# Shorter edge lists and moved list transfers in a sparse graph attention kernel

## The chip, the cores and the metric

The kernel runs on one core of one Trainium2 chip. The metric is the device time of one execution in microseconds; less is better. Times of a kernel are given as the median of several runs with the lowest and highest beside it.

## What is computed

The reference is one layer of graph attention with a feed-forward part, on 4096 nodes of 512 features, 8 heads of 64. `adj` is a 4096 by 4096 matrix of int32 with ones where there is an edge; it is symmetric and its diagonal is one. Cut to what matters:

```python
hs = layer_norm(x);  ht = layer_norm(h_target)          # 4096 x 512 each
q, k, v = ht @ Wq + bq, hs @ Wk + bk, hs @ Wv + bv      # heads of 64
logits = where(adj != 0, q k^T / 8, -1e30)              # 4096 x 4096 per head
ht = ht + softmax(logits) v @ Wo + bo
ht = layer_norm(ht)
y  = ht + gelu(ht @ W1) @ W2                            # 512 -> 2048 -> 512
out = layernorm(x + y)
```

A row of `adj` has 17.05 ones on average, 5 at the least and 35 at the most (counted in the seeded inputs). So of the 4096 keys of a row only some 17 count, and the kernel never forms the dense logits: it makes a list of the neighbours of every row and gathers their keys and values.

## The kernel before

All tiles are 128 rows; there are 32 of them. The work has these parts.

**Projections.** Every tile of `x` is loaded through the sync queue, normalized, transposed on TensorE and multiplied by Wk and Wv (L930). ScalarE copies the result out of PSUM (L932), and a DMA of ScalarE's queue writes the 128 rows of keys and values, 512 KB, to a table `kvd` in DRAM (L936).

**Edge lists** (`edges`, L717 on). For each tile of 128 rows the adjacency comes in four quarter rows of 1024 int32, 512 KB each, by DMAs of the sync queue (`quarter`, L714). ScalarE turns a quarter into 1024 bytes of 0 or 1 and sums them to the row's degree (L729). VectorE reads the bytes as 512 pairs of 16 bits, multiplies each by its position in its segment, counted in columns (`lio`, L734), and takes the eight largest of every segment (MAX8, L736). A quarter row has `SQ` = 5 segments of at most 103 pairs (`WS`), so `SEG` = 20 segments a row give 160 candidates. At the end of a tile the low and high bytes of the candidates are taken apart (L743, L744), the offset of the segment is added where the byte is not zero (L748, L751), and from the 320 numbers the 24 largest are drawn by three MAX8 and two MATCH_REPLACE8 (L755, L757). They are the ids of the neighbours, plus one, and stand in the row's record. The rest of the 320 is written to DRAM (`rest_d`, L767, sync queue, in the middle of the next tile's edges) for the few rows with more than 24 neighbours, which read it back later (`rest_of`).

**Sorts.** The rows are sorted by degree in two halves (tiles 0 to 15 and 16 to 31), so that a tile of the sorted order needs only as many neighbour slots as its largest row (`CAPS_A`, `CAPS_B`; 11 to 39). `sort(part)` works out the rank of each row and scatters the records, 116 bytes each, of each of its 16 tiles to DRAM by an indirect DMA of GpSimd's queue (L854): 16 scatters in a sort.

**Attention.** For a sorted tile, `prefetch` loads the 128 records (L980, GpSimd's queue; six buffers, `rec`), asked for two tiles ahead. `front` gathers the rows of `h_target` and makes the queries. `issue` gathers the keys and values of one neighbour slot for 128 rows at a time (`gather`, L967: 603 of them for keys and values), three slots to a step, into a ring of 17, later 20, slots, four or five steps ahead. VectorE multiplies keys by queries (L1220) and sums them to logits (L1225), ScalarE takes the exponential (L1229) and scales one slot of the step (L1204), VectorE the other two (L1184), and TensorE adds the weighted values by transposes into PSUM (L1192), which frees the ring's slots. `finish` divides, multiplies by Wo, and normalizes.

**Feed-forward** (`feed`). Groups of two tiles go through W1 (L1325), Gelu on ScalarE (L1328) and W2 (L1334); `end` normalizes and scatters the rows to the output (L1302).

**Order.** Streams of the program are generators that `_weave` runs by costs: after each piece a stream tells a cost, and the stream with the smallest sum goes next. First the projections, the lists of the first 16 tiles with the first sort, and the lists of five more tiles (`fill`) are woven; then attention, feed-forward, and `other_lists` (the last 11 tiles' lists and the second sort). That gives the program order. A scheduler then orders each engine's queue when the kernel is compiled: by program order where instructions are ready in its own reckoning, so that a ready one may pass an earlier one that isn't. Each queue is executed in order: a waiting instruction holds what stands behind it. Gathers, scatters, the records' loads and a small power instruction (L687, for the normalizations) all stand in GpSimd's queue.

At its end the kernel checks flags (each row's count of ids against its degree, and the like). If one is set, a dense general path runs as well.

Of the kernel before, what the change touches and what calls it, by code (L numbers as in the profile page):

```python
# [1 line left out]

# [10 lines left out]
ALU = mybir.AluOpType  # L13
# [4 lines left out]
P = 128  # L18
# [360 lines left out]
RW = E0 + RE  # L379
# [5 lines left out]
def _order():  # L385


    n, m = len(CAPS_A), len(CAPS_B)
    a = [(k * P, c) for k, c in enumerate(CAPS_A)]
    b = [((n + k) * P, c) for k, c in enumerate(CAPS_B)]  # L390
    groups = [[a.pop()]]
    while len(a) > 1:
        groups.append([a.pop(), a.pop()])
    groups.append(a + [b.pop()])
    while len(b) > 1:
        groups.append([b.pop(0), b.pop()])
    return groups + [b]
# [46 lines left out]
def adj_resnorm_kernel(  # L444
# [33 lines left out]
    nc = tc.nc  # L478
# [9 lines left out]
    NQ = 4  # L488
    QW = N // NQ
    WQ = QW // 2  # L490
    SQ = 5
    WS = -(-WQ // SQ)
    SEGS = [(s * WS, min(s * WS + WS, WQ)) for s in range(SQ)]
    SEG = NQ * SQ
    groups = _order()
# [17 lines left out]
    recs_d = [dram.tile([n * P, RW], I32, name=f"rec{i}") for i, (_, n) in enumerate(PARTS)]  # L513
# [19 lines left out]
    with tc.tile_pool(name="keep", bufs=1) as keep:  # L533
# [17 lines left out]
        with ExitStack() as late:  # L551
# [50 lines left out]
            cnt = lp.tile([P, NT], F32, name="cnt")  # L602
            segoff = lp.tile([P, 2, NQ, SQ], F32, name="segoff")
            lio = lp.tile([P, WQ], U16, name="lio")
# [3 lines left out]

            def list_constants():
                io = turn_of("wide", wide)  # L610
                nc.gpsimd.iota(io[:, :SQ * WS], pattern=[[0, SQ], [2, WS]], base=1,
                               channel_multiplier=0)

                nc.vector.tensor_copy(lio, io[:, :WQ])
                io = turn_of("wide", wide)
                nc.gpsimd.iota(io[:, :2 * SEG], pattern=[[1, 2], [QW, NQ], [2 * WS, SQ]], base=0,
                               channel_multiplier=0)
                nc.gpsimd.iota(io[:, 2 * SEG:2 * SEG + NB], pattern=[[1, NB]], base=0,
                               channel_multiplier=0)

                nc.vector.tensor_copy(segoff.rearrange("p b q s -> p (b q s)"), io[:, :2 * SEG])
                nc.vector.tensor_copy(bins, io[:, 2 * SEG:2 * SEG + NB])

                nc.gpsimd.memset(lower, -1.0)
                nc.gpsimd.affine_select(out=lower, in_=lower, compare_op=ALU.is_ge, fill=0.0,
                                        base=0, pattern=[[-1, P]], channel_multiplier=1)
                for R, (i0, n) in zip(Rs, PARTS):
                    nc.gpsimd.memset(R, 0)
                    for c, base in ((TGT, i0 * P), (ROW, 0)):
                        nc.gpsimd.iota(R[:, :, c], pattern=[[P, n]], base=base,  # L630
                                       channel_multiplier=1)
                nc.vector.memset(one_c, 1.0)
# [76 lines left out]
            def quarter(i, h):  # L709
                if i < RINGED:  # L710
                    a = ring[:, (i * NQ + h) % DEEP, :].bitcast(I32)
                else:
                    a = turn_of("wide", wide)
                nc.sync.dma_start(a, adj[i * P:(i + 1) * P, h * QW:(h + 1) * QW])  # L714
                return a

            def edges(i):  # L717

                part = 1 if i >= NA else 0
                rec = Rs[part][:, i - PARTS[part][0], :]  # L720
                cand = lp.tile([P, SEG, 8], U16, name="cand", bufs=2)
                for h in range(NQ):
                    n = i * NQ + h
                    while len(adjs) < min(n + 2, NT * NQ):
                        adjs.append(quarter(*divmod(len(adjs), NQ)))
                    a, adjs[n] = adjs[n], None

                    sg = turn_of("signs", signs)
                    nc.scalar.activation(sg, a, AF.Sign, accum_out=dpart[:, i, h:h + 1])  # L729
                    ahead = min(n + DEEP - 1, n + 3 + n // 2)  # L730
                    while len(adjs) < min(max(n + 3, min(ahead, RINGED * NQ)), NT * NQ):
                        adjs.append(quarter(*divmod(len(adjs), NQ)))
# [12 lines left out]
                gid = lp.tile([P, 2 * SEG, 8], F32, name="gid")  # L745
                dec = dec.rearrange("p b s e -> p (b s) e")
                off = segoff.rearrange("p b q s -> p (b q s)")
                nc.vector.scalar_tensor_tensor(gid, dec, 0.0,  # L748
                                               off.unsqueeze(2).to_broadcast([P, 2 * SEG, 8]),
                                               op0=ALU.is_gt, op1=ALU.mult)  # L750
                nc.vector.tensor_add(gid, gid, dec)  # L751
                flat = gid.rearrange("p s e -> p (s e)")
                for r in range(RE // 8):
                    top = rec[:, E0 + r * 8:E0 + (r + 1) * 8]
                    nc.vector.max(top, flat)  # L755
                    if r + 1 < RE // 8:
                        nc.vector.match_replace(flat, top, flat, 0.0)  # L757
                held.append((rest_d[i * P:(i + 1) * P, :], flat))
                has = lp.tile([P, MAXE], F32, name="ehas")
                nc.vector.tensor_scalar(has[:, :RE], rec[:, E0:E0 + RE], 0.0, 0.0, op0=ALU.is_gt,  # L760
                                        op1=ALU.add, accum_out=cnt[:, i:i + 1])
                yield 4.0

            def keep_rest():

                while held:
                    nc.sync.dma_start(*held.pop())  # L767
# [40 lines left out]
            def sort(part):  # L808
# [3 lines left out]
                pool, R = lp, Rs[part]  # L812
# [3 lines left out]
                ranki, b16 = tools[:, 960:960 + n].bitcast(I32), tools[:, 976:984].bitcast(BF16)  # L816
                nc.vector.scalar_tensor_tensor(dif, deg[:, me], float(RE), cnt[:, me], op0=ALU.min,
                                               op1=ALU.not_equal)
                nc.vector.tensor_reduce(bad[:, 1 + part:2 + part], dif, AX.X, ALU.max)
                nc.vector.tensor_scalar(dif, deg[:, me], 0.0, float(NB - 1), op0=ALU.max,  # L820
                                        op1=ALU.min)
# [14 lines left out]
                for c in range(2):  # L836
# [5 lines left out]
                                                 op0=ALU.mult, op1=ALU.add)  # L842
# [8 lines left out]
                nc.vector.tensor_copy(ranki, rank)  # L851
                yield 10.0
                for i in range(n):
                    ins = nc.gpsimd.indirect_dma_start(  # L854
                        out=recs_d[part][:, :],
                        out_offset=bass.IndirectOffsetOnAxis(ap=ranki[:, i:i + 1], axis=0),
                        in_=R[:, i, :], in_offset=None)

                    tc.declare_no_dep(ins.ins, group=f"scatter{part}", reason="other rows")
                    tc.add_to_no_dep_group(f"scatter{part}", ins.ins)  # L860
                    yield 3.0 if part else 1.3
# [99 lines left out]
                        yield cost  # L961


            recs, tqs, h2Ts, done, ready, latest, newest = {}, {}, {}, set(), [], [], []

            def gather(dst, table, idx):
                nc.gpsimd.indirect_dma_start(  # L967
                    out=dst, out_offset=None, in_=table[:, :],
                    in_offset=bass.IndirectOffsetOnAxis(ap=idx, axis=0))

            def prefetch(i):
                if i >= NT or i in recs:
                    return
                r0 = TILES[i][0]
                part = 1 if r0 >= PARTS[1][0] * P else 0
                assert part in done
                r0 -= PARTS[part][0] * P
                rec = sp.tile([P, E0 + MAXE], I32, name="rec", bufs=6)

                nc.gpsimd.dma_start(rec[:, :RW], recs_d[part][r0:r0 + P, :])  # L980
                recs[i] = rec

            def front(i, idle=0):
# [503 lines left out]
```

## Time and profile before

| what | value |
|---|---|
| median of 3 runs | 1815.98 us (1813.75 to 1820.42) |
| profiled execution, its time | 1817.49 us |
| its span in the profile | 1815.5 us |
| TensorE matmul busy | 1677.8 us, 92% |
| VectorE busy | 1436.5 us, 79% |
| ScalarE busy | 1224.1 us, 67% |
| GpSimd busy | 982.2 us, 54% |
| mean granted TensorE clock | 0.967 |
| DMA | 463.26 MB, 255 GB/s on the mean |

The profile is that of one execution. A share of busy time is a mean over stages with different limits, so the stages are looked at one by one: the projections with the first lists up to some 296 us, the start of attention up to 380 us, attention beside the last 11 tiles' lists up to some 600 us, the second sort's scatters between 627 and 665 us, attention with feed-forward up to 1650 us, and the tail. In the lists below, "[a <-b]" after an instruction is the time that its engine sat idle before it, and what ended the wait. L numbers are lines of the kernel.

### The profile page before, as it was taken

How to read it: one execution, taken by the hardware profiler on the slowest of the kernel's cores; microseconds unless marked ns; L12 is line 12 of the kernel's file. 1: busy time of each engine (PE TensorE's matmuls, PEld its weight loads, DVE VectorE, ACT ScalarE, POOL GpSimd, SP SyncE). 2: the span in 40 equal slices, each digit the busy share in tenths (PEclk: the TensorE clock that was granted, in tenths of full speed). 3: DMA queues.
4: the chain of work that ended last, by engine and by line, in shares of the span. 5: the costliest groups of instructions: out<-in, count | busy, mean ns of one | idle time of the engine just before them, and what ended most of it. 6: DMA issues, size and time to landing. Idle time of an engine off the chain costs nothing. (4 is left out here: it accounts for less than half of the span.)

```text
span 1815.5 us, 22973 instructions
## 1 busy us (share of the span) xinstructions
PE 1677.8 (92%) x7030; PEld 1097.9 (60%) x7030; DVE 1436.5 (79%) x2660; ACT 1224.1 (67%) x3121; POOL 982.2 (54%) x834
## 2 busy tenths in 40 slices
PE   7989984597999979999999989999999999999997
PEld 3434442465766656766776757666666666666664
DVE  6989876899999837777978989978878797988200
ACT  5767654487987736766778868877777676787311
POOL 1000144656566676766678788867575665763101
PEclk9999996698999989999999999999999999999998
DMA  9999968989887557777878878787776776774000
GB/s 344 366 380 372 344 198 319 404 287 332 271 305 256 201 173 243 258 255 267 273 263 302 293 260 295 249 285 250 241 266 222 248 251 238 244 248 153 18 6 26
DMA packets 140269, 463.26 MB, mean 255 GB/s; under 512 B 16500, under 2 KB 21672, under 8 KB 140136
## 3 DMA queue, kind: packets, MB, share of 16 engines
q0 software_dynamic: 96656, 342.64, 55.8%
q1 hardware_dynamic: 35664, 95.98, 15.0%
q10 hardware_dynamic: 7816, 23.08, 3.3%
q8 instruction: 58, 0.95, 0.2%
q14 instruction: 75, 0.61, 0.1%
HBM read 430.75 MB, written 30.89 MB: 254 GB/s over the span
## 5 line engine op out<-in xcount | busy, mean ns | idle before, releaser
L967 POOL DMA_INDIRECT kv<-kvd,rec x603 | 758.1, 1257 | 347.5 <-PE cps L1192 139.7
L1334 PE MATMUL po<-w,gt 128*128 128x512 f32 x1024 | 466.4, 598 | 16.2 <-ACT gt L1328 16.2
L1325 PE MATMUL pf<-h2T,w 128*128 128x256 f32 (+1 forms) x2176 | 465.9, 368 | 0.1
L1325 PEld LDWEIGHTS pf<-h2T,w 128*128 128x128 f32 x2176 | 389.3, 191 | 64.5 <-issue 20.3
L1220 DVE TENSOR_TENSOR kv<-kv,tq 128x1536 f32<-128x1536 f32 (+2 forms) x211 | 351.6, 1675 | 68.3 <-DMA kv<-kvd,rec 56.2
L1204 ACT ACTIVATE kv<-kv,pa 128x64 f32<-128x64 f32 x1520 | 391.0, 336 | 4.3
L1225 DVE TENSOR_REDUCE lg<-kv 128x24 f32<-128x1536 f32 (+2 forms) x211 | 350.1, 1666 | 1.4
L1334 PEld LDWEIGHTS po<-w,gt 128*128 128x128 f32 x1024 | 188.8, 192 | 212.4 <-issue 194.3
L1192 PEld LDWEIGHTS cps<-ident,kv 128*128 128x128 f32 x2008 | 240.2, 145 | 109.4 <-issue 59.2
L1192 PE MATMUL cps<-ident,kv 128*128 128x128 f32 x2008 | 264.5, 280 | 44.1 <-DVE kv L1184 24.5
L1184 DVE TENSOR_TENSOR kv<-kv,p 128x1024 f32<-128x1024 f32 (+1 forms) x211 | 251.0, 1193 | 22.8 <-ACT p L1229 20.3
L687 POOL TENSOR_TENSOR n_rs<-n_ve,mhalf 128x2 f32<-128x2 f32 (+2 forms) x51 | 50.8, 997 | 329.1 <-DVE n_ve L680 165.3
L729 ACT ACTIVATE kv<-kv 128x1024 uint8<-128x1024 int32 x128 | 134.9, 1056 | 100.0 <-DMA kv<-in_adj_dram 51.7
L1328 ACT ACTIVATE gt<-pf 128x512 f32<-128x512 f32 x128 | 76.4, 597 | 93.8 <-PE pf L1325 75.8
L1328 ACT ACT_TABLE_LOAD x104 | 133.4, 1283 | 1.7
L736 DVE MAX8 cand<-kv 128x8 uint16<-128x103 uint16 (+1 forms) x640 | 131.8, 252 | 0.8 <-DVE R L755 0.2
L930 PE MATMUL pq<-wk,h2T 128*128 128x512 f32 x256 | 120.8, 616 | 12.1 <-ACT tq L932 7.2
L1012 PE MATMUL t<-wq,tq 128*128 128x512 f32 x256 | 118.2, 605 | 5.6 <-ACT tq L1006 5.6
L930 PE MATMUL pq<-wv,h2T 128*128 128x512 f32 x256 | 115.5, 594 | 6.4 <-ACT kv L729 3.0
L1229 ACT ACTIVATE p<-lg 128x24 f32<-128x24 f32 (+2 forms) x179 | 39.2, 219 | 113.0 <-DVE lg L1225 88.8
L1116 PE MATMUL t<-wo,rb 128*128 128x512 f32 x256 | 115.2, 592 | 0.0
L930 PEld LDWEIGHTS pq<-wk,h2T 128*128 128x128 f32 x256 | 48.9, 197 | 69.9 <-issue 55.2
(160 smaller groups left out, 1582.2 us busy)
## 6 DMA issues: line engine op xcount, KB each, us to landing
kv<-in_adj_dram SPq DMA_DIRECT2D x128, 512.0 KB
kvd<-tq ACTq DMA_DIRECT2D x24, 512.0 KB
kv<-kvd,rec POOLq DMA_INDIRECT x603
kv<-in_L_gnn_h_target_dram SPq DMA_DIRECT2D x32, 256.0 KB
kv<-in_x_dram SPq DMA_DIRECT2D x15, 512.0 KB
rest_d<-gid SPq DMA_DIRECT2D x32, 160.0 KB
w<-in_L_gnn_W_dram SPq DMA_DIRECT2D x4, 1024.0 KB
kvd<-kv ACTq DMA_DIRECT2D x8, 512.0 KB
```

The lines of the kernel that those rows point to most:

```text
L729: nc.scalar.activation(sg, a, AF.Sign, accum_out=dpart[:, i, h:h + 1])
L736: nc.vector.max(cand[:, h * SQ + s, :], wd[:, w0:w1])
L930: nc.tensor.matmul(pkv, hT[:, kc, j * P:(j + 1) * P], w[:, kc, :], start=kc == 0, stop=kc == KC - 1)
L967: nc.gpsimd.indirect_dma_start(out=dst, out_offset=None, in_=table[:, :], in_offset=bass.IndirectOffsetOnAxis(ap=idx, axis=0))
L1184: nc.vector.tensor_tensor(v4, v4, p[:, j0:j0 + m, :].unsqueeze(3) .to_broadcast([P, m, H, HD]), ALU.mult)
L1192: nc.tensor.matmul(cps[:, c, :], kv[:, j, D + c * P:D + (c + 1) * P], ident, is_transpose=True, start=j0 + j == 0 and c == 0, stop=j0 + n ...
L1204: newest[:] = [nc.scalar.mul(v, v, pa[:, hd:hd + 1]).ins]
L1220: nc.vector.tensor_tensor(kv[:, :n, :D], kv[:, :n, :D], tq[:, :D].unsqueeze(1).to_broadcast([P, n, D]), ALU.mult)
L1225: nc.vector.tensor_reduce(lg[:, :n, :], kv[:, :n, :D].rearrange("p j (h d) -> p j h d", h=H), AX.X, ALU.add)
L1325: nc.tensor.matmul(pf[:, k, :], w1[(f0 + k) // KC][:, kc, (f0 + k) % KC * P:((f0 + k) % KC + 1) * P], h2T[:, kc, :w], start=kc == 0, stop= ...
L1328: nc.scalar.activation(gt, pf, AF.Gelu_apprx_tanh)
L1334: nc.tensor.matmul(po[j], gt[:, k, j * P:(j + 1) * P], w2[(f0 + k) // KC][:, (f0 + k) % KC, :], start=False, stop=f0 + k == FC - 1, skip_g ...
```

## The change

It has three parts.

1. A quarter row has three segments (`SQ` = 3) of at most 171 pairs where it had five of 103. So that positions still fit in a byte, the multiplier counts pairs (1 to 171) and no longer columns, and the id is put together as twice the byte plus the offset, which is one smaller; the ids are the same as before. A row has 12 segments, 96 candidates and 192 numbers to draw from, and `rest_d` has 192 columns.
2. Each scatter of a sort is put behind the last gather before it in program order, if there was one (`behind`; `issues` holds that gather). The first sort comes before any gather, so it is left as it was; in the second, a scatter can't be queued ahead of that gather.
3. The records of the second half's tiles are loaded through the sync queue; those of the first half through GpSimd's, as before.

```diff
-    SQ = 5
+    SQ = 3
...
-                nc.gpsimd.iota(io[:, :SQ * WS], pattern=[[0, SQ], [2, WS]], base=1,
+                nc.gpsimd.iota(io[:, :SQ * WS], pattern=[[0, SQ], [1, WS]], base=1,
...
-                nc.gpsimd.iota(io[:, :2 * SEG], pattern=[[1, 2], [QW, NQ], [2 * WS, SQ]], base=0,
+                nc.gpsimd.iota(io[:, :2 * SEG], pattern=[[1, 2], [QW, NQ], [2 * WS, SQ]], base=-1,
...
+            def behind(ins):
+                return tc.issue_after(ins[-1]) if ins else nullcontext()
...
-                nc.vector.tensor_add(gid, gid, dec)
+                nc.vector.scalar_tensor_tensor(gid, dec, 2.0, gid, op0=ALU.mult, op1=ALU.add)
...
-                    ins = nc.gpsimd.indirect_dma_start(
-                        out=recs_d[part][:, :],
+                    with behind(issues):
+                        ins = nc.gpsimd.indirect_dma_start(
+                            out=recs_d[part][:, :],
...
             def gather(dst, table, idx):
-                nc.gpsimd.indirect_dma_start(
+                issues[:] = [nc.gpsimd.indirect_dma_start(
                     out=dst, out_offset=None, in_=table[:, :],
-                    in_offset=bass.IndirectOffsetOnAxis(ap=idx, axis=0))
+                    in_offset=bass.IndirectOffsetOnAxis(ap=idx, axis=0)).ins]
...
-                nc.gpsimd.dma_start(rec[:, :RW], recs_d[part][r0:r0 + P, :])
+                (nc.sync if part else nc.gpsimd).dma_start(rec[:, :RW], recs_d[part][r0:r0 + P, :])
```

More of the change, by code (lines that the diff above doesn't have):

```diff
@@ L1 @@
-from contextlib import ExitStack
+from contextlib import ExitStack, nullcontext
 import concourse.bass as bass
@@ L853, in sort @@
                 for i in range(n):
-                    ins = nc.gpsimd.indirect_dma_start(
-                        out=recs_d[part][:, :],
-                        out_offset=bass.IndirectOffsetOnAxis(ap=ranki[:, i:i + 1], axis=0),
-                        in_=R[:, i, :], in_offset=None)
+                    with behind(issues):
+                        ins = nc.gpsimd.indirect_dma_start(
+                            out=recs_d[part][:, :],
+                            out_offset=bass.IndirectOffsetOnAxis(ap=ranki[:, i:i + 1], axis=0),
+                            in_=R[:, i, :], in_offset=None)
                     tc.declare_no_dep(ins.ins, group=f"scatter{part}", reason="other rows")
@@ L961, in project @@
                         yield cost
-            recs, tqs, h2Ts, done, ready, latest, newest = {}, {}, {}, set(), [], [], []
+            recs, tqs, h2Ts, done, ready, latest, newest, issues = {}, {}, {}, set(), [], [], [], []
             def gather(dst, table, idx):
-                nc.gpsimd.indirect_dma_start(
+                issues[:] = [nc.gpsimd.indirect_dma_start(
                     out=dst, out_offset=None, in_=table[:, :],
-                    in_offset=bass.IndirectOffsetOnAxis(ap=idx, axis=0))
+                    in_offset=bass.IndirectOffsetOnAxis(ap=idx, axis=0)).ins]
             def prefetch(i):
```

## The prediction

> **What bounds the kernel now.** I read the busy times by stage first, since the shares of the whole span mix stages with different limits.
>
> ```profile
> core 0: us, PE busy (x) PEld busy (x) DVE busy (x) ACT busy (x) POOL busy (x), PEclk, DMA share, GB/s
> 20.00:200.00 180.00, 172.77 (x462) 80.64 (x461) 168.24 (x736) 130.87 (x241) 11.34 (x15) 0.98 1.00 368
> 200.00:296.00 96.00, 73.80 (x196) 33.73 (x195) 71.98 (x305) 55.80 (x108) 29.01 (x29) 0.93 0.78 261
> 296.00:380.00 84.00, 47.54 (x216) 34.50 (x215) 69.09 (x93) 41.90 (x142) 60.24 (x49) 0.71 0.95 364
> 380.00:600.00 220.00, 208.78 (x979) 145.35 (x978) 212.64 (x466) 176.91 (x439) 128.27 (x108) 0.97 0.85 293
> 600.00:700.00 100.00, 88.74 (x403) 61.27 (x402) 62.62 (x71) 61.58 (x164) 69.04 (x60) 0.95 0.57 191
> 700.00:1650.00 950.00, 924.70 (x4119) 635.79 (x4118) 802.87 (x873) 702.69 (x1907) 661.43 (x538) 0.99 0.78 260
> ```
>
> PE holds the end: from 380 us on it is busy 1374.8 of 1426 us. So a gain can only come out of PE's idle time and of time at a low clock. Idle PE time by stage: 7.2, 22.2, 36.5, 11.2, 11.3, 25.3 us. VectorE is full where lists are made (93% from 20 to 200 us, 97% from 380 to 600 us) and at 85% or less elsewhere after 600 us. Next the timelines of GpSimd (its last line is a record load of the second half), VectorE and PE around the second sort:
>
> ```profile
> 627.06 1.01 POOL L854 DMA_INDIRECT rec<-R,kv  x1 [1.53 <-DVE kv L851]
> ...
> 638.89 0.96 POOL L854 DMA_INDIRECT rec<-R,kv  x1 [0.30 <-issue]
> ...
> 652.48 1.41 POOL L854 DMA_INDIRECT rec<-R,kv  x1 [0.30 <-issue]
> ...
> 887.25 0.58 POOL L980 DMA_DIRECT2D rec<-rec  x1 [5.28 <-DVE n_ve L680]
> ```
>
> ```profile
> 664.35 1.76 DVE L1220 TENSOR_TENSOR kv<-kv,tq 128x1536 f32<-128x1536 f32 x1 [9.37 <-DMA kv<-kvd,rec]
> ```
>
> ```profile
> 671.55 5.51 PE L1334 MATMUL po<-w,gt 128*128 128x512 f32 x8 [9.95 <-ACT gt L1328]
> ```
>
> Nine scatters stand in a row from 627.06 us, three gathers follow, then six more; VectorE then waits for gathered keys, ScalarE's exponential waits for VectorE's logits, the Gelu stands behind it in ScalarE's queue, and PE waits 9.95 us for the Gelu. The sync queue is free by then; its list of waits has
>
> ```profile
> SPq L1453 <- DVE flag L1372: 1222.8, 1, 1222.8
> ```
>
> that is, nothing from some 584 us to the end but a wait for the last flag.
>
> [...]ten MAX8 of 103 run from 223.09 to 224.77 us, 168 ns from start to start[...]; the MAX8 of 320 at 195.24 us is followed 0.41 us later[...]. [...]a record load costs GpSimd 0.593 us on the mean here. [...]after the 9.95 us above, eight matmuls took 5.51 us, where eight without a wait take 3.60.
>
> **Part 1, three segments.** MAX8 of 171 isn't in the trace. [...]A quarter row falls from 5 x 168 = 840 to 3 x 238 = 715 ns, 0.125 us; a tile of four by 0.50 us. Bounds: no dearer than in proportion (280 ns, no gain), no cheaper than the 168 of 103 elements (1.34 us a tile). I take 0.50[...]. At the end of a tile seven operations (L748, L751, three L755, two L757) go from 320 to 192 elements: 394 to 260 ns, 7 x 0.133 = 0.93 us. Their floor is no gain, their ceiling proportion, 7 x 0.158 = 1.10 us. L751 becomes a scalar_tensor_tensor like L748, which took 482 ns to its 476, so nothing. L743 and L744 start 0.11 us apart; I give them 0.04 us together. Sum 1.47 us a tile, 47 us over 32. Of these, 16 tiles (23.5 us) fall before 200 us, five (7.4) up to about 380, eleven (16.2) between 380 and 583 us. `rest_d` shrinks from 160 to 96 KB: over 21 tiles 1.34 MB, at 368 GB/s 3.6 us of transfer. The read-back of rest rows happens twice and counts nothing. No list loses an edge: in this adjacency no segment of 171 has more than eight pairs with an edge.
>
> How much comes through:
> - 20 to 200 us: VectorE goes from 168 to 145 us and stops being full. PE can win no more than its 7.2 us idle, and transfers already run at 368 GB/s where the page's best slice has 404 (66.2 MB would take 164 us, so up to 16 us). I take 4 us.
> - 200 to 296 us: PE's 22.2 us are waits for ScalarE, whose queue waits 23.3 us in sum for adjacency quarters; these wait for buffers and stand behind `rest_d` in the sync queue, which waits for VectorE. VectorE is freed of 7 us, PE gets perhaps 3. The first gathers (296.58 us) then start 7 us earlier. Bounds of these two items: 20 us gained (all but a third of 29.4), 20 lost (see the rival).
> - 296 to 380 us: VectorE waits for gathers (11.0 us), transfers run at 364 GB/s. Nothing; if fewer list loads are left for this stage, up to 5.
> - 380 to 600 us: 16 us off a full VectorE, against 11.2 us of PE idle and about 4 of low clock. PE has feed-forward work to cover the rest, so I take a third, 5 us. Without that cover it would be the full 15; zero if PE's short waits are ScalarE's own.
>
> **Part 2, the pinned scatters.** No instruction is added. A scatter costs 1.26 to 1.31 us of GpSimd from start to start, 16 of them 20 us, and still has to be paid. By the costs in program order a scatter comes every 3 units, and a slot costs 60/34 = 1.76 of them, so one scatter to 1.7 gathers over some 27 gathers. GpSimd then needs 27 x 1.25 + 16 x 1.28 + about 8 other issues x 1.25 = 64 us for 48 units; a unit is some 75/60 = 1.25 us at PE's pace, 60 us. The ring's lead of four steps (12 gathers) covers the 4 us short. What a scatter now waits for is the gather ahead of it, behind it wait gathers and L687, as before. The first of the second half's records was loaded at 749.20 us, 85 us after the last scatter, so a later end of the sort hides. Removed: 9.95 us of PE idle and 1.9 of slow clock; I keep back 4 for smaller waits: 8 us. Bounds: 0 (scatters stay together) to 12; if the lead runs out several times, 5 lost.
>
> **Part 3, records through the sync queue.** GpSimd loses 16 x (0.593 + 0.3 of gap) = 14 us of issue, and the waits in front of two of them, 5.28 us at 887.25 and 2.25 us at 1013.69 us, no longer hold the gathers behind. SP gets 16 issues of about 0.33 us (what `rest_d` costs it) and waits there for a free `rec` buffer and the scatters; behind it stand only later records. A record needs to be there one to two tiles later, 40 us or more. From 700 us PE idles 25.3 us; only part is for gathers, so 2 us; bounds 0 and 8.
>
> Sum: 4 + 3 + 0 + 5 + 8 + 2 = 22 us. The profiled execution took 1817.49 us, 2 us outside its span, so 1795.5; its time is 1.5 us above the median of the runs. Forecast 1795.
>
> **Rivals.**
> - Pins without effect. If ranks come late (1.53 us waited at 627.06), the gathers that scatters stand behind may be long issued, and the scatters still run in a row. For it: the program place of the sort, 258 units, is near tile 8, which was being finished when it ran, at 630 us. Against: only nine ran together, so others had their place later. Part 2's 8 us are lost: 1803.
> - Hidden anyway. PE is 97% busy in 20 to 200 us as it is, transfers hold the first stage, and ScalarE's own chain the later ones: part 1 gives 2 us, parts 2 and 3 give 2. For it: DMA share 1.00. Against: PE's waits at 431 and 442 us fall where VectorE is full. 1812.
> - Slower: ScalarE's queue. With VectorE cheaper, the scheduler may put adjacency passes (L729) further ahead of the copies of projections (L932), and the transfers can't follow. Already the last value copy runs at 289.99 us, though its matmuls ended at 280.6, behind three passes. If waits of L729 for adjacency from 200 to 296 us double, from 23.3 to 47 us, the first gather moves to about 320 us, and with 8 us kept later the time is 1831. It decides from 15 us or so of added delay. Against: a freed VectorE also frees sign buffers and `rest_d` sooner.
>
> **How the numbers follow.** A measurement tells about 0.5%, 9 us, from no change. Chances: likeliest 0.45, pins without effect 0.18, hidden 0.21, slower 0.16. Likeliest's own range is 1780 to 1806. Faster than 1807: nearly all of the first, most of the second, a little of the third: 0.61; slower than 1825: 0.15; within, 0.24. The range's low end takes the first two items at their bound of 20 for my 7, and 5 us more of the other upper bounds: 1795 - 18 = 1777. Above it reaches into the slower case, to 1827.
>
> **What would show it.** MAX8 x384 near 238 ns start to start; VectorE near 145 us in 20 to 200; first gather before 292 us; scatters apart with gathers between, no PE wait near 10 us after them; 16 record loads on SP, none on POOL after 700 us. Wrong if the first gather comes after 300 us, if scatters run six or more together, or if PE's idle time after 380 us stays at 51 us.

## The result, and the profile after

The changed kernel takes 1831.44 us (median of 6 runs, 1825.6 to 1834.01), the kernel before in the same comparison 1817.67. The ratio is 1.0063 (95% interval 1.0045 to 1.008): 0.6% slower, where 1795 us was forecast, and above the range of 1777 to 1827. The profiled execution took 1830.23 us, its span is 1828.5 us (1815.5 before).

The busy times by stage of the changed kernel, in the columns of the view shown for the kernel before:

```profile
core 0: us, PE busy (x) PEld busy (x) DVE busy (x) ACT busy (x) POOL busy (x), PEclk, DMA share, GB/s
20.00:200.00 180.00, 173.50 (x463) 81.13 (x462) 152.36 (x614) 130.59 (x243) 15.33 (x15) 0.98 1.00 370
200.00:296.00 96.00, 80.81 (x207) 36.68 (x205) 64.81 (x251) 58.67 (x113) 31.08 (x36) 0.93 0.80 267
296.00:380.00 84.00, 47.58 (x251) 38.33 (x252) 73.06 (x92) 47.30 (x151) 58.26 (x46) 0.76 0.97 364
380.00:600.00 220.00, 197.08 (x894) 135.48 (x893) 187.80 (x381) 159.82 (x410) 117.32 (x100) 0.95 0.76 266
600.00:700.00 100.00, 97.67 (x440) 66.14 (x439) 70.70 (x75) 63.62 (x171) 65.33 (x56) 1.00 0.62 200
700.00:1650.00 950.00, 922.74 (x4101) 635.70 (x4100) 799.83 (x872) 704.03 (x1910) 652.85 (x530) 0.99 0.78 260
```

VectorE lost 16 us of work up to 200 us and 25 us between 380 and 600 us, the latter in part because less of attention's work was done there. PE did not follow: from 200 to 296 us it did 7.0 us more, from 380 to 600 us 11.7 us less (197.08 for 208.78). VectorE was no longer full there (85%), so over the stage as a whole it was not what held PE. From 600 to 700 us PE is almost never idle (2.3 us), and from 700 to 1650 us it did 2.0 us less.

A sharper reading: from the first attention tile on, PE's matmuls stand in nearly the same order in both kernels, so the k-th matmul of a line in one trace can be set against the k-th in the other. The difference in start times is PE's lead (negative) or lag (positive) against the profile of before; "at 305 us" stands for the last matmul that had begun by 305 us in the profile of before. For the changed kernel it is -9.1 us at 305 us (the products with Wq, L1012, for the first tiles), -2.3 at 515 us, +9.7 at 530 us, -2.3 at 680 us, +10.1 at 730 us, +4.1 from 1400 us to the last matmul, and +13.0 at the end of the span. So there are seven terms: 9.1 won early, 6.8 given back by 515 us, 12.0 lost within 15 us, 12.0 won near 671 us, 12.4 lost again between 697 and 728 us, 6.0 won slowly, and 8.9 lost after the last matmul.

**The loss at 527 us.** PE's waits, in a timeline of the changed kernel; before, PE ran through this stretch with one wait of 1.40 us:

```profile
527.06 0.48 PE L1147 MATMUL t<-ident,h 128*128 128x128 f32 x1 [5.41 <-ACT h L1138]
...
534.38 1.12 PE L1103 MATMUL t<-ident,rb 128*128 128x128 f32 x4 [3.16 <-ACT h2T L1151]
```

ScalarE's timeline of the changed kernel, from which the passes over the adjacency (L732, L729 before) and the copy of h (L1125) are picked:

```profile
494.40 1.04 ACT L732 ACTIVATE kv<-kv 128x1024 uint8<-128x1024 int32 x1
...
496.81 1.06 ACT L732 ACTIVATE kv<-kv 128x1024 uint8<-128x1024 int32 x1
...
502.82 1.06 ACT L732 ACTIVATE kv<-kv 128x1024 uint8<-128x1024 int32 x1 [4.86 <-DMA kv<-in_adj_dram]
...
505.77 1.05 ACT L732 ACTIVATE kv<-kv 128x1024 uint8<-128x1024 int32 x1
...
508.27 1.06 ACT L732 ACTIVATE kv<-kv 128x1024 uint8<-128x1024 int32 x1 [1.36 <-DVE cand L739]
...
514.88 1.06 ACT L732 ACTIVATE kv<-kv 128x1024 uint8<-128x1024 int32 x1 [5.46 <-DVE lg L1229]
...
518.91 0.56 ACT L1125 COPY h<-t 128x512 f32<-128x512 f32 x1
```

Six passes stand in a row between two steps of attention, and three of them wait. The view puts two of these waits down to VectorE, but in the raw records each of the three ends with the landing of the pass's own adjacency quarter, about 0.1 us ahead of it (502.71, 508.17 and 514.78 us). Behind the row stands the copy of h, whose matmuls ended near 508 us; on it hang the normalization, h's transposes and the next feed-forward group. Before, the same stretch of ScalarE's queue had two passes, and ScalarE had stood idle for 0.50 us when PE's h came (timeline of ScalarE, before):

```profile
510.58 0.58 ACT L1121 COPY h<-t 128x512 f32<-128x512 f32 x1 [0.50 <-PE t L1116]
```

There are two buffers for adjacency quarters at this time, so a row of passes goes no faster than quarters come in: each of the three was issued when an earlier pass had freed its buffer and landed 4.2 to 7.8 us later.

**The loss at 697 to 728 us.** The scatters did spread: 16 of them from 636.31 to 724.73 us, never more than two without another issue between, and PE's wait of 9.95 us at 671 us is gone. VectorE still waits for gathered keys, 10.41 and 3.00 us where it waited 9.37 and 7.95 before; the longer wait is

```profile
675.86 1.76 DVE L1224 TENSOR_TENSOR kv<-kv,tq 128x1536 f32<-128x1536 f32 x1 [10.41 <-DMA kv<-kvd,rec]
```

But the Gelu that PE needs now runs at 669.57 us, ahead of the exponential that waits for these keys (679.44 us), and PE works through. Then comes this, in the timelines of GpSimd, VectorE and PE of the changed kernel:

```profile
708.61 0.62 POOL L984 DMA_DIRECT2D rec<-rec  x1
709.23 0.76 POOL L687 TENSOR_TENSOR n_rs<-n_ve,mhalf 128x2 f32<-128x2 f32 x1
713.21 1.05 POOL L971 DMA_INDIRECT gid<-rest_d,rec  x1 [3.22 <-DMA rec<-rec]
```

```profile
710.03 0.16 DVE L692 SCALAR_TENSOR_TENSOR n_nm<-mv,n_rs 128x2 f32<-128x2 f32 x1 [7.77 <-issue]
...
716.03 0.09 DVE L782 MATCH_VALUE_LOAD gid<-rec,gid 128x8 int32 x1 [5.85 <-DMA gid<-rest_d,rec]
```

```profile
717.50 1.11 PE L1147 MATMUL t<-ident,h 128*128 128x128 f32 x4 [5.15 <-DVE tq L1021]
...
727.28 2.82 PE L1196 MATMUL cps<-ident,kv 128*128 128x128 f32 x12 [2.70 <-DVE kv L1188]
```

From 666.5 us on GpSimd goes from one instruction to the next with no wait over 0.31 us, and the power instruction (L687) comes out of its queue late; its input was there at 702.25 us, it ran at 709.23, and VectorE stood for it 7.77 us. The record of a tile that has rest rows was loaded at 708.61 us; the read-back of the rest rows waits for it, and VectorE for the read-back, 5.85 us. The same instructions in the kernel before, in the timelines of GpSimd and VectorE:

```profile
695.50 0.58 POOL L980 DMA_DIRECT2D rec<-rec  x1 [4.50 <-DVE p L1083]
...
702.40 0.73 POOL L687 TENSOR_TENSOR n_rs<-n_ve,mhalf 128x2 f32<-128x2 f32 x1
```

```profile
703.17 0.16 DVE L692 SCALAR_TENSOR_TENSOR n_nm<-mv,n_rs 128x2 f32<-128x2 f32 x1 [2.99 <-issue]
...
705.42 0.09 DVE L779 MATCH_VALUE_LOAD gid<-rec,gid 128x8 int32 x1 [2.09 <-DMA gid<-rest_d,rec]
```

**The loss after the last matmul.** The last output scatter is issued at 1810.78 us (1806.68 before); the span ends 17.7 us later (8.8 before). In the lists of waits the sync engine's wait in the closing section is, first for before, then for the change (us in total, times, longest; the wait is put down to PE's sequencer, but what ends last in the raw records is an instruction of GpSimd named DRAIN, called the drain below, 1.95 and 9.30 us):

```profile
SPq L1482 <- PEq L1482: 2.0, 2, 1.4
```

```profile
SPq L1486 <- PEq L1486: 9.3, 2, 8.8
```

### The profile page after: what moved, and what is told of

It is laid out like the page before. It is cut to its first block, busy times and chain, and to the rows that moved or that the text cites. A ratio compares the mean times of both kernels' runs of the same rounds, so it can differ in the third digit from the quotient of the medians.

```text
span 1828.5 us, 22815 instructions
## 1 busy us (share of the span) xinstructions
PE 1686.4 (92%) x7030; PEld 1103.2 (60%) x7030; DVE 1400.0 (77%) x2404; ACT 1218.8 (67%) x3117; POOL 964.2 (53%) x818
## 5 line engine op out<-in xcount | busy, mean ns | idle before, releaser
L687 POOL TENSOR_TENSOR n_rs<-n_ve,mhalf 128x2 f32<-128x2 f32 (+2 forms) x51 | 50.6, 993 | 345.5 <-DVE n_ve L680 192.9
L732 ACT ACTIVATE kv<-kv 128x1024 uint8<-128x1024 int32 x128 | 134.8, 1055 | 109.7 <-DMA kv<-in_adj_dram 62.2
L739 DVE MAX8 cand<-kv 128x8 uint16<-128x171 uint16 (+1 forms) x384 | 111.5, 325 | 1.0
```

## The experiments

Leads (-) and lags (+) of PE against the profile of before, in us, read as above. "Span" is the whole span's difference, so the last two columns differ in the main by what happens after the last matmul. The leads of a kernel come from one profiled execution, which was not always a typical one: it took the most time of the kernel's runs in e_seg and e_hold, and the least in e_seg_hold and e_spread4. Medians and ratios come from all runs. The kernel before was run again in each comparison; its medians were 1817.7 us beside the changed kernel, 1815.2 beside e_seg, e_pin, e_sync and e_seg_sign4, 1814.3 beside e_seg_hold, e_hold, e_sync_last and e_pin_rec, 1817.2 beside e_seg_h30, e_after_last, e_pin_rec17 and e_best, and 1815.3 beside the last two. In the names, seg is the shorter lists, pin the pinned scatters, and sync or rec records through the sync queue; each is described where it comes up.

| kernel | median us | ratio (95%) | 305 | 515 | 530 | 690 | 730 | 1500 | span |
|---|---|---|---|---|---|---|---|---|---|
| changed kernel | 1831.4 | 1.0063 (1.0045 to 1.008) | -9.1 | -2.3 | 9.7 | -2.3 | 10.1 | 4.1 | 13.0 |
| e_seg | 1820.7 | 1.0028 (1.0016 to 1.004) | -8.6 | -0.9 | 11.0 | 11.3 | 10.1 | 11.8 | 11.5 |
| e_pin | 1814.0 | 0.9997 (0.9984 to 1.0011) | -8.8 | -5.2 | -4.9 | -16.9 | -4.1 | -6.5 | -6.8 |
| e_sync | 1819.1 | 1.0023 (1.0011 to 1.0035) | -3.3 | -3.6 | -3.5 | -3.7 | -3.4 | -6.3 | 2.3 |
| e_seg_sign4 | 1825.7 | 1.0049 (1.0033 to 1.0066) | -9.9 | -5.2 | 9.0 | 9.4 | 7.9 | 9.4 | 9.3 |
| e_seg_hold | 1831.3 | 1.0091 (1.0068 to 1.0113) | -8.0 | 5.8 | 10.6 | 11.6 | 11.6 | 11.0 | 11.0 |
| e_hold | 1841.5 | 1.0138 (1.011 to 1.0166) | -4.7 | 23.2 | 22.3 | 29.4 | 29.6 | 33.2 | 33.3 |
| e_sync_last | 1811.5 | 0.9984 (0.9965 to 1.0003) | -1.5 | 1.1 | 1.1 | 1.6 | 1.6 | -4.0 | -5.5 |
| e_pin_rec | 1814.1 | 0.9993 (0.998 to 1.0005) | -1.4 | -0.6 | -1.0 | -13.1 | -3.3 | -9.7 | -1.6 |
| e_seg_h30 | 1818.9 | 1.0009 (0.9996 to 1.0023) | -10.0 | -4.4 | -0.2 | -0.3 | -1.2 | -1.3 | 0.1 |
| e_after_last | 1820.9 | 1.002 (1.0001 to 1.0039) | -11.3 | -6.6 | 4.2 | -7.9 | 3.7 | -2.2 | -3.6 |
| e_pin_rec17 | 1804.2 | 0.9933 (0.9918 to 0.9949) | -1.4 | 1.4 | 1.1 | -10.9 | -2.4 | -8.9 | -10.5 |
| e_best | 1807.5 | 0.9953 (0.9938 to 0.9969) | -10.3 | -4.2 | 0.1 | -11.9 | -3.8 | -10.6 | -12.0 |
| e_spread4 | 1801.1 | 0.9919 (0.9898 to 0.9941) | -4.5 | -1.3 | -1.3 | -13.3 | -12.5 | -20.3 | -20.5 |
| e_spread5 | 1802.1 | 0.9926 (0.9905 to 0.9946) | -2.2 | 0.8 | 0.9 | -11.1 | -11.3 | -13.9 | -15.4 |

### Each part alone

The shorter lists alone (the diff's lines on `SQ`, the two iotas and the id):

> Only the shorter lists (three segments), no pins, records of the second half through GpSimd's queue as before. Theory A, ScalarE's queue: an adjacency pass that waits for a sign buffer holds the copy that PE needs, because VectorE's cheaper lists have shifted the order. Then the loss is in this part alone: the first weighted-value matmul comes 8 to 10 us earlier than before, and PE falls back by about 12 us near 525 us, where it waits over 4 us for the copy of h; the 9.95 us wait for the Gelu near 671 us stays; time within 4 us of before, or up to 10 more with the longer drain at the end. Theory B, the pins and the sync queue's records changed the order elsewhere: this part keeps its lead of 7 to 10 us to the end, 1808 us, and no wait for h over 4 us near 525 us. On the drain of GpSimd at the end (9.3 us after the change, 2.0 before): 2 us if the records on the sync queue cause it.

The pins alone (`behind` and `issues`):

> Only the pinned scatters. If they work as forecast, PE loses its 9.95 us wait near 671 us and nothing takes its place: 1808 to 1810 us. If the loss only moves (a scatter between gathers makes the gathers late, as the changed kernel's waits at 697 to 728 us suggest), PE is about 12 us ahead at 690 us and back at zero by 730 us: within 3 us of before, 1815 to 1821. If theory B holds, PE already falls back near 525 us in this kernel: 1825 or more.

The record loads alone:

> Only the second half's records through the sync queue. Forecast of the prediction: 2 us faster, bounds 0 and 8, all of it after 750 us. If this part causes the long drain of GpSimd at the end, the drain takes about 9 us where it took 2, the span's end comes 9 us later after the last output scatter, and the time is 5 to 9 us longer, 1822 to 1826. If the drain varies from run to run or comes from another part, 1812 to 1818.

Each loss has its part. The jump at 527 us (11.9 us) is in the shorter lists alone and in neither of the others: theory A in its place (but not in its reason, that a pass waits for a sign buffer), theory B out. The pins win 12.0 us at 671 us and lose 12.8 by 730 us; time unchanged. The sync queue's records win 2.9 us after 730 us and bring the long drain, 9.30 us as in the changed kernel; the other two keep 1.95 us. Two times were not as expected: e_seg is 5.5 us over before without a longer drain (within 4 expected), and e_sync, at 1819.1 us, is 3.9 over it (1822 to 1826 expected). The three ratios add up to 1.0048 for the whole change's 1.0063.

### What holds ScalarE's queue

A fourth buffer for the signs beside the shorter lists:

```diff
+            signs.append(kp.tile([P, QW // 4], F32, name="sign4").bitcast(U8))
...
-                cand = lp.tile([P, SEG, 8], U16, name="cand", bufs=2)
+                cand = lp.tile([P, SEG, 8], U16, name="cand", bufs=1)
```

> The shorter lists with a fourth buffer for the signs (1 KB a partition more; the candidates have one buffer, which VectorE alone writes and reads). Theory A: an adjacency pass then seldom waits for VectorE's MAX8, the wait for the copy of h near 525 us falls under 2 us, and PE keeps 7 us or more of its lead: 1807 to 1811 us. If the passes wait for the adjacency itself (the transfers or the sync queue), the fourth buffer changes nothing: within 3 us of the kernel with the shorter lists alone.

It changed nothing for the better: PE loses 14.2 us there, and the time is no less (5 us over e_seg's median, where within 3 was expected). Sign buffers are not the cause. With the fourth buffer the scheduler placed seven passes in that row, and the passes waited for their quarters (5.41 us for the first that waits, and by the raw records for the later ones as well). So the next two kernels changed the row itself, the same edit with and without the shorter lists:

```diff
-                    nc.scalar.activation(sg, a, AF.Sign, accum_out=dpart[:, i, h:h + 1])
+                    with behind(newest):
+                        nc.scalar.activation(sg, a, AF.Sign, accum_out=dpart[:, i, h:h + 1])
```

> The shorter lists, and every adjacency pass queued behind the last value scaling of ScalarE that comes before it in program order, so that passes can't be pulled ahead of attention's work; ScalarE's queue then has at most three passes between two steps of attention instead of six. If the row of six passes, each waiting for its adjacency quarter, is what costs 12 us of PE near 525 us, PE has no wait over 3 us for h there, keeps 4 us or more of the early lead and the time is 1806 to 1812 us, 11 us or more under the kernel with shorter lists alone. If the loss comes from VectorE (the lists standing between attention's steps), it is as large or only moves: 1817 to 1825.

> The kernel before with the same order for the passes and nothing else. It had four passes at most in a row, and none where PE was short of cover, so the order alone should be worth little: within 5 us of before. If it gains as much as it does with the shorter lists, then the order is good by itself and the shorter lists give nothing; if the kernel with both is still 4 us or more under this one, the shorter lists are worth that.

Both misses, and no clean test: the edit holds back all 128 passes, those of the first stage behind the last write of keys and values. By 296 us 82 passes have run, where 94 had before and 96 with the shorter lists, and the rest falls on attention's first steps. PE now loses 14 us between 350 and 380 us (-12.6 to +1.8) with the shorter lists, and some 27 us between 305 and 440 us (-4.7 to +22.2) with five segments. The loss at 515 to 530 us did shrink, to 4.8 us and to nothing. The narrow form holds only the passes of tiles 30 and 31:

```diff
-                    with behind(newest):
+                    with behind(newest if i >= 30 else []):
```

> The shorter lists, with the adjacency passes of the last two tiles alone queued behind the last value scaling of ScalarE ahead of them in program order. ScalarE's queue is the same as with the shorter lists alone up to the row of six passes; of the six, two stay and four come later, one to three at a time. If the row of six is what costs PE 12 us near 525 us, then up to 500 us PE stands as in that kernel, some 1 to 5 us ahead of before, and from 530 us it still stands no worse than 4 us behind before (11.0 behind with the row): 1808 to 1814 us. If VectorE's order or the adjacency transfers themselves cost it, PE falls 8 us or more there and the time is 1818 to 1822.

ScalarE's queue is unchanged up to the row, of which two passes stay. PE comes in at -4.4 and leaves at -0.2 us: 4.2 us lost, where 11.9 were. The copy of h is back at its time (timeline of ScalarE), and PE's only wait over 1 us from 505 to 545 us is this one:

```profile
509.39 0.56 ACT L1125 COPY h<-t 128x512 f32<-128x512 f32 x1
```

```profile
525.23 1.11 PE L1103 MATMUL t<-ident,rb 128*128 128x128 f32 x4 [3.92 <-issue]
```

So the row of passes is shown to be the cause of some 8 of the 12 us. The other traces agree: from 515 to 530 us the four with the row lose 10.8 to 14.2 us, the two in which it is broken this way 4.2 and 4.3, and those with five segments, e_hold apart, 0.3 at most. In the medians the edit is worth less, 0.19% or 3.4 us, with intervals that overlap, and the time, 1818.9, misses the 1808 to 1814 expected; part of that is that before itself stood at 1817.2 in that comparison.

### The drain at the end

The last tile's record back on GpSimd's queue, first with the third part alone:

```diff
-                (nc.sync if part else nc.gpsimd).dma_start(rec[:, :RW], ...)
+                (nc.sync if part and i < NT - 1 else nc.gpsimd).dma_start(rec[:, :RW], ...)
```

> The second half's records through the sync queue, all but the last tile's, which stays on GpSimd's queue. If GpSimd's long drain at the end comes from having had no plain transfer of its own queue since 700 us, it is 2 us again (9.3 with all on the sync queue), and the time is 6 to 9 us under that kernel: 1810 to 1813 us. If it comes from the sync queue's part in the records, or from the number of plain transfers on GpSimd's queue, the drain stays at 8 us or more and the time at 1817 to 1820.

The drain is 0.73 us, less even than the 1.95 of before, and the ratio falls from 1.0023 to 0.9984. But the reason expected is wrong: in before and in this kernel alike, 115 indirect transfers (gathers and scatters) follow GpSimd's last plain one, and the drains differ; and the pinned kernel with early records (below) also has a late plain one and drains 8.98 us. What fits is the number of transfers that GpSimd's queue issues in the whole kernel:

| transfers on GpSimd's queue | kernels | drain ns | semaphore instruction ahead of it, ns |
|---|---|---|---|
| 745 | e_pin_rec | 8975 | 2375 |
| 749 | changed kernel, e_sync | 9302 | 2455 |
| 750 | e_sync_last | 727 | 360 |
| 765 | before, e_seg, e_pin and four more | 1952 | 660 |

From 745 to 749 and from 750 to 765, each further transfer adds 82 ns to the drain and 20 ns to the instruction ahead of it (327/4, 1225/15; 80/4, 300/15); between 749 and 750 both fall. All these kernels have the same 733 indirect transfers, so it can't be told whether they count or the plain ones alone. This was put to two kernels, the whole change with the last record back on GpSimd's queue, and the early records with 17 loads left there, 750 transfers in each:

> The whole change, with the record load of the last tile back on GpSimd's queue, so that this queue issues 750 transfers where it issued 749. By the count of transfers (82 ns of drain for each one[...]; 745 gave 8.98 us, 749 gave 9.30, 750 gave 0.73, 765 gave 1.95) the drain at the end is 0.73 us and the time 7 to 10 us under the changed kernel's 1831: 1821 to 1824 us. If the 0.73 us in the other kernel was of another cause, the drain is 8 us or more and the time 1829 to 1832.

> Five segments as before, the pinned scatters, and the records of tiles 11 to 25 through the sync queue: 17 loads stay on GpSimd's queue, 750 transfers in all (745 with the records of tiles 11 to 30 on the sync queue). By the count the drain is 0.73 us instead of 8.98, the rest stays as it was, and the time is 7 to 9 us under that kernel: 1805 to 1808 us. If the long drain there came from the number of sync queue records, it falls little, and the time is 1812 or more.

Both drain in 727 ns, as the count had it, and so do the three kernels with 750 transfers below. The whole change falls to 1820.9 us (ratio 1.002 for 1.0063), the other kernel from 1814.1 to 1804.2 (0.9933 for 0.9993). So from 749 to 750 transfers, the program's end becomes 10.7 us shorter (8.58 in the drain, 2.10 in the instruction ahead of it). What makes them fall there isn't shown.

### What takes the pins' gain

The pinned kernel with the records of tiles 11 to 30 on the sync queue, so that the record of the tile with rest rows doesn't stand behind GpSimd's scatters and gathers:

```diff
+                (nc.sync if 11 <= i < NT - 1 else nc.gpsimd).dma_start(rec[:, :RW], ...)
```

> The pinned scatters, and the records of the sorted tiles 11 to 30 through the sync queue. The pinned kernel lost its 12 us again at 697 to 720 us: VectorE waited 6.5 us for the small power instruction and 6.1 us for the read-back of rest rows, whose record load had come late in GpSimd's queue. If the late record is half of it, the second wait goes and PE keeps 5 us or more of the 12 past 720 us: 1806 to 1810 us with a short drain. If the backlog of GpSimd's queue is all of it, the loss stays at 10 us or more: 1812 to 1816.

VectorE's wait for the read-back falls from 6.06 us in the pinned kernel to 2.09, its wait for the power instruction's result stays (6.51 and 8.39). PE keeps 2.3 us of its 12.1 by 730 us (-1.0 at 530 us, -3.3 then), where the pinned kernel ends up 0.8 behind: less than the 5 expected. The rest should then be the backlog of GpSimd. It was tested on e_pin_rec17 by spreading the same scatters further, to 4 and to 5 units of program order:

```diff
-                    yield 3.0 if part else 1.3
+                    yield 4.0 if part else 1.3
```

> As the best kernel so far (five segments, pinned scatters, records of tiles 11 to 25 through the sync queue), with the scatters of the second sort 4 units apart in program order instead of 3, 64 units in all for 48. If the loss at 700 to 720 us is GpSimd's backlog (the small power instruction stands behind scatters and gathers, VectorE waits 7.2 us for it), the backlog is smaller by some 5 to 10 us of issue when that instruction comes, VectorE waits under 4 us for it, PE keeps 3 us or more of what it lost there (8.1 us), and the time is 1799 to 1803 us. If the power instruction is late for another reason (what feeds it is late), the wait stays at 6 us or more, and the time at 1804.

> The same with 5 units, 80 units in all. By the backlog theory the wait is no longer than with 4 units, and the time 1798 to 1803 us, unless the later end of the sort now holds the first records of the second half: these were loaded near 745 us, and the last scatter would run near 755 us; then VectorE waits for gathers near 770 us and the time is 1806 or more. By the other theory, 1804 or more as well, with the wait for the power instruction at 6 us or more.

Now PE stands at -13.3 and -11.1 us at 690 us and at -12.5 and -11.3 at 730 us: the gain is kept. From 680 to 722 us VectorE waits 1.49 us for what the power instruction feeds (7.16 in e_pin_rec17); it still waits 7.26 us for the read-back of rest rows, but PE runs through that. In the timelines of e_spread4, GpSimd stands idle again (5.37 us) ahead of the read-back: by the raw records it waits for the tile's record, which the sync queue issued at 682.17 us and which landed at 686.42. So the backlog is gone, the power instruction runs 0.7 us after its input is there (6.4 in e_pin_rec17), and PE's one wait over 1 us from 660 to 790 us is in the last line:

```profile
687.34 0.96 POOL L971 DMA_INDIRECT gid<-rest_d,rec  x1 [5.37 <-issue]
...
694.66 0.72 POOL L687 TENSOR_TENSOR n_rs<-n_ve,mhalf 128x2 f32<-128x2 f32 x1
```

```profile
705.82 1.53 PE L1196 MATMUL cps<-ident,kv 128*128 128x128 f32 x12 [2.33 <-DVE kv L1188]
```

The later end of the sort (722.44 and 753.31 us) costs nothing up to 790 us. From there to 850 us the seven kernels with records on the sync queue and 3 units win 3.5 to 4.9 us, e_spread4 0.5, and e_spread5 loses 2.1, so a price may lie there; it was not tested. Nor is the gain clear of noise in the times: they are as expected, but the ratios, 0.9919 and 0.9926, differ from the 0.9933 of e_pin_rec17 by less than their intervals. With 1801.1 us, ratio 0.9919 (0.9898 to 0.9941), e_spread4 has the lowest median of this study, 0.8% under before: five segments, pins 4 units apart, the records of tiles 11 to 25 on the sync queue, 750 transfers on GpSimd's.

### Whether the shorter lists are worth anything

> All together: three segments, the last two tiles' adjacency passes held back, pinned scatters, records of tiles 11 to 25 through the sync queue, 750 transfers on GpSimd's queue. If the gains add up (early lists about 6 us, pins with early records about 8, a drain of 0.73 us for 1.95), 1798 to 1803 us. If the row of six passes was not the cause of the loss near 525 us, or the later sort makes its scatters late, 1808 or more.

The edits together with three segments: 1807.5 us, not the 1798 to 1803 expected, and not under the 1804.2 of the same edits with five segments, run beside it. The trace shows where the lists' gain goes. PE starts attention at -10.3 us against -1.4, is at -4.2 against 0.6 at 420 us, and at 0.1 against 1.1 at 530 us. What the early lists win, PE has given back by 530 us, while the last lists are being made.

## Why the prediction was wrong, and where it was right

**Durations: right.** MAX8 of 171 elements takes, in VectorE's timeline,

```profile
223.29 1.52 DVE L739 MAX8 cand<-kv 128x8 uint16<-128x171 uint16 x6
```

1.52 us for six, each 0.32 to 0.33 long: (1.52 - 0.33)/5 = 238 ns from start to start. That is my estimate, to the nanosecond. At the end of a tile MAX8 and MATCH_REPLACE8 went from 0.39 us to 0.26 from one start to the next (medians; in before one MAX8 started at 193.90 us and the next instruction at 194.29, in the changed kernel one at 183.36 and the next at 183.62), where I had put 394 and 260 ns. A straight line through before's two sizes of MAX8, 168 ns at 103 elements and 0.39 us at 320, gives 238 ns at 171 and 0.26 us at 192. VectorE's work up to 200 us fell to 152, not 145 us.

**20 to 296 us, 7 us: right, but not to be read from one pair of profiles.** The first gather for attention came at 287.26 us, 9.3 us earlier. But the kernels with five segments, e_hold apart, have the same order in every queue up to 500 us, and PE's lead at 305 us lies anywhere between 0 and -8.8 us in them: the profile of before was the latest of eight (mean -2.9). The seven kernels with three segments lie between -8.0 and -11.3 (mean -9.6). The difference of the means is 6.7 us.

**380 to 600 us, 5 us: the step that failed first.** Its bounds were 0 and 15. I took VectorE as the limit and PE's short waits as its doing, and did not put a loss into the range. In fact the cheaper lists moved passes in ScalarE's queue: from 380 to 600 us PE lost 16.6 us (-6.9 to +9.7), 12.0 of them at 515 to 530 us, and some 8 of these are shown to be the row's. PE's idle time after 380 us did not fall, as the prediction's own sign of being wrong has it: it is 55.8 us up to the last output scatter's start, where 51.2 were. The slower rival named this mechanism, passes ahead of ScalarE's other work, but for the projections from 200 to 296 us. There the waits for the adjacency did grow, from 23.3 to 30.4 us, and PE still came earlier; the mechanism struck 230 us later, where two adjacency buffers are left. That the rival's time, 1831 us, is the one measured is luck: its first gather would have come at about 320 us, and 8.9 us of the measured loss lie behind the last matmul. Where I named its place, I should have asked it of each stage in which the same queue holds both kinds of work.

**Part 2, 8 us: the gain was right, its keeping wrong.** The pins did what was said and won 12 us at 671 us, the upper bound. The slow clock behind the wait went with it: in before the eight matmuls behind it took 5.51 us, at a granted clock of 0.67 from 671.5 to 677.2 us; the changed kernel's eight at 671.12 us took 3.60, at 1.00. The step that failed is that "the ring's lead of four steps (12 gathers) covers the 4 us short", and in it the remark that gathers and L687 wait behind a scatter "as before". The shortage itself was mis-sized. I priced a gather at 1.25 us from start to start, the usual case; the mean in before is 1.57 (gathers after 300 us with no wait behind them), since some take longer, and the nine scatters in a row took 1.46 each for my 1.28. In the changed kernel the stretch from the first scatter to the last holds 57 instructions of GpSimd and lasts 88.4 us, 9.9 of them waits: 78 us of work for the 64 forecast. The lead did not cover that for VectorE (its wait of 10.41 us for keys), though PE had other work by then. And nothing covers the instructions of GpSimd that have no lead: the power instruction, wanted at once by VectorE, and a record load whose read-back is wanted soon. I had not asked what stands in GpSimd's queue at the moment when something urgent comes. The bounds given, 5 lost to 12 won, held it; the value taken from between them did not.

**Part 3, 2 us: right in place, blind to the end.** GpSimd's 16 loads went, the sync queue took them at 0.32 us each (0.33 forecast), and PE gained 2.9 us after 730 us in e_sync, 6.0 in the changed kernel. Over all traces the nine kernels with records on the sync queue win 2.6 to 7.8 us from 730 to 1500 us (5.6 on the mean), the other seven between 2.4 won and 3.6 lost (0.5 lost on the mean), so the gain is real and nearer 6 us than 2. The step that failed is the cost that is missing: GpSimd's transfers were priced at their issue alone, and the end of the program at nothing. The profile of before shows the 2.0 us wait of the closing section, and no view of it tells that it depends on their count. It cost 9.15 us (7.35 in the drain, 1.80 in the instruction ahead of it), more than the part gains.

**296 to 380 us, nothing:** it gave back 2.2 us of the lead (-9.1 to -6.9). The sum by measured terms: 6.7 won early for 7; 2.2 lost for 0; 380 to 600 us 16.6 lost for 5 won; the pins 0.4 lost for 8 won; the records 6.0 won for 2, and 8.9 lost at the end. That is 15.4 us lost, where the two spans differ by 13.0; the 2.4 between are the part of the early lead (9.1 for 6.7) that is before's own spread.

**What stays open:** what makes PE give back 4 us near 525 us with three segments even when the row is broken; why it waits for a Gelu near 406 us in the traces with three segments that keep the early order (0.3 to 3.2 us; after the three waits of 2.59 us and more the eight matmuls behind took 5.28 to 5.40 us for 3.70, so that 4.6 to 5.2 us of the lead went there; five of the kernels with five segments lose 1.4 to 1.9 us at this place too); and what makes GpSimd's drain fall between 749 and 750 transfers.

## What to carry to other kernels

An operation made cheaper can change the order in which a scheduler fills the other queues (here six passes in a row for two): compare how many of the moved kind now stand in a row ahead of the copy that the bound engine needs, in every stage. Before spreading transfers through a queue, list what else in it has no lead, and move or thin out until the queue waits again (here with the scatters 4 units apart VectorE waited 1.49 us for what the power instruction feeds, with 3 units 7.16). And set matmul k against matmul k between two traces: seven terms of 6 to 12 us that largely cancel show up at once, where busy times by stage blur them.

## What the runs showed that I had not expected

- GpSimd's drain at the end of the program grew by 82 ns, and the semaphore instruction ahead of it by 20 ns, for each further transfer of its queue (745 to 749, 750 to 765), and both fell between 749 and 750: 9.30 and 2.46 us with 749 transfers, 0.73 and 0.36 us with 750.
- Executions of one order of instructions differ by up to 8.8 us at 305 us; at 515 us they still differ by up to 6.6 us (-5.2 to +1.4).
- A fourth buffer made a row of waiting passes longer (seven for six) instead of shorter.
